# Layer 3: two row scans in one instruction, steps of 511 and half columns, decay in four fixed banks, another order of PE's pieces

## The chip, the cores and the metric

The kernel runs on one core of a Trainium2 chip, in float32 throughout. The metric is the device time of one launch in microseconds (us), the median of several runs. One further execution was recorded by the profiler; its page and its trace are what the profile lines below come from. Engines are named as the profile does: PE is TensorE's matmul and PEld its weight load, DVE is VectorE, ACT is ScalarE, POOL is GpSimd, SP is the engine that issues most DMAs.

## The reference

Four residual layers work on x of 2 x 192 x 96 x 96, each on a group-normalised x: a deformable convolution block, a Laplacian with a 1x1 convolution, a two-way WKV block, and a Mamba block. Only the last is touched by the change:

```
xz = x_flat @ W_in.T;  x_in, z_gate = split(xz)          # 192 -> 2 x 384 channels
x_conv = silu(causal depthwise conv of 4 taps(x_in) + conv_b)
dt, B_ssm, C_ssm = split(W_x x_conv, [12, 16, 16])
delta = softplus(W_dt dt + 2 b_dt);   A = -exp(A_log)    # A: 384 channels x 16 states
for t:  h = exp(delta_t A) * h + (delta_t x_conv_t) B_t ;  y_t = sum over the 16 states of h C_t
y = (y + D x_conv) * silu(z_gate);   x = x + W_out y
```

The loop over t has 9216 steps in each of two batches; h starts at zero in each batch.

## The kernel before

Layer 3 cuts each batch into 18 steps `s` of 512 columns (positions t), 36 in all. The 384 x 16 rows of h are worked in 12 groups `q` per step (counter `k` = 12 s + q), each of 4 x 128 rows: partition p holds a state and one of 8 channels, `r` = 0 to 3 picks a further channel. For one group:

- `load` (L2322): SP loads `bu`, 128 x (4 x 512), from the DRAM tile `ud` that holds delta * x_conv; each of its rows goes to 16 partitions. `times_b` (L2330, POOL) multiplies it by the rows `bs` of B.
- `steps_of` (L2339, PE): four matmuls of 32 x 512, one for each 32-row part of the array, spread delta over the states, each into a PSUM bank of the pool `da` of five. `decay` (L2353, ACT): exp of it, in place, with the scale `nA`.
- `scan` (L2363, DVE): four scans of 512 columns, h = da * h + bu, that start from a column of `state` (0 at a batch's start). `keep` (L2370, ACT) copies the last column to `state`.
- `times_c` (L2386, DVE) multiplies three of the rows by `cc`, the rows of C in PSUM; `times_c_aside` (L2397, POOL) multiplies the fourth. `sum_of` (L2410, PE) sums over the states into `acc`, two groups later; `skip` (L2404) adds D x_conv; `gate` (L2423, DVE) makes `y` at every fourth group.

What prepares a step are generators. `early` (two steps ahead): `xn` on ACT, 6 projections `w_in` of two matmuls each (L2231), evicted to `xi` or `zs`, 3 convolutions of four `taps` matmuls (L2251), evicted to `us`, then Silu of `zs` and `us`. `late` (one step ahead): `wx` (L2266) to `xd`, whose rows go through DRAM to `bs` and `cs`; 3 `wdt` matmuls (L2290), each evicted twice, to `du` and `dl`; then softplus: Exp and Identity on ACT, L2300 on DVE, Ln on ACT, L2303, L2305 and L2307 on POOL, and the store of `ud`. `output` (for the step before): load of `xr`, two times three `w_out` matmuls (L2435), each followed by an addition on DVE (L2443), and the store. All of these matmuls share one PSUM bank, `pe`; with `cc`, `acc` and the five `da` that is eight.

The order on PE, ACT, DVE and POOL is the order of the program (`manual_schedule`): nothing overtakes on an engine's queue. The loop over `k` draws the next part from a generator at given q: `AHEAD` ahead of the sums and scans, `BEHIND` after the scans and between `steps_of` and `decay` of the next group. ACT has to load a table of functions when it passes between Exp, Ln and Silu (a row of its own, 1.28 us). SP issues DMAs in its own order, each when its wait is over.

Of the kernel before, what the change touches and what calls it, by code (L numbers as in the profile page):

```python
# [9 lines left out]
ALU = mybir.AluOpType  # L10
# [53 lines left out]
class Net:  # L64
# [2021 lines left out]
    def layer3(self, x, out, stats):  # L2086
# [4 lines left out]
        T = 512  # L2091
        NC = HW // T
# [5 lines left out]
        with ExitStack() as ctx:  # L2098
# [81 lines left out]
            pa = ctx.enter_context(tc.tile_pool(name="l3a", bufs=5, space=PSUM))  # L2180
# [9 lines left out]
            tail = wp.tile([P, ND, 3], F32, name="tail")  # L2190
            ctx.enter_context(
# [9 lines left out]
            steps = [(b, c) for b in range(B) for c in range(NC)]  # L2201
            ns = len(steps)
            got = {}

            def bank():
                return ps.tile([P, T], F32, name="pe")

            def early(s):

                b, c = steps[s]  # L2210
                xt = sb.tile([CH, 2, T], F32, name="xt")
                nc.sync.dma_start(out=xt, in_=halves(x[b])[:, :, c * T : (c + 1) * T])
                xn = s1.tile([CH, 2, T], F32, name="xn")
# [5 lines left out]
                us = s3.tile([P, ND, T], F32, name="us")  # L2219
                zs = s3.tile([P, ND, T], F32, name="zs")  # L2220
                xi = s1.tile([P, ND, T + 3], F32, name="xi")
                got[s] = {"us": us, "zs": zs}
                if c == 0:
                    nc.gpsimd.memset(tail, 0.0)
                nc.scalar.copy(xi[:, :, 0:3], tail)
                yield

                def project(at):
                    pe = bank()
                    for k in range(2):  # L2230
                        nc.tensor.matmul(  # L2231
                            pe, w_in[:, k, at : at + P], xn[:, k], start=k == 0, stop=k == 1
                        )
                    return pe

                for d in range(ND):
                    pe = project(d * P)
                    yield
                    nc.scalar.copy(xi[:, d, 3:], pe)  # L2239
                    if d == ND - 1:  # L2240
                        nc.scalar.copy(tail, xi[:, :, T : T + 3])
                    yield
                for d in range(ND):
                    pe = project(DI + d * P)
                    yield
                    nc.scalar.copy(zs[:, d], pe)
                    yield
                for d in range(ND):
                    pe = bank()
# [371 lines left out]
```

## Time and profile before

| | |
|---|---|
| median of 3 runs | 10371.55 us (10369.88 to 10373.33) |
| the profiled execution | 10376.11 us, span 10373.9 us |
| busy in the span: PE, DVE, ACT, POOL | 88%, 80%, 58%, 67% |
| layer 3's preparation, first projection to first scan | 7063.7 to 7182.8 us |
| its loop, first scan to the last product `hc` | 7182.8 to 10358 us |
| its end, to the end of the span | 15.5 us |
| in 7182.4 to 10360: PE, DVE, ACT, POOL busy | 2985, 2925, 1902, 2815 of 3178 us |

A line of the page's groups gives the source line, the engine, the operation, output and inputs with their shapes, the count, then busy us, mean ns of one, and the idle time just before them with what ended most of it. An fp32 matmul is recorded as two passes. In the rows by stages, PEclk is the share of TensorE's full clock that was granted.

### The profile page before, as it was taken

To read this page: it belongs to the slowest core of one execution; us is meant where nothing else is said; L and a number is where in the kernel's file an instruction comes from. 1 tells how busy PE (TensorE), PEld (TensorE's weight loads), DVE (VectorE), ACT (ScalarE), POOL (GpSimd) and SP (SyncE) were. 2 spreads that over 40 slices of the span, in tenths; PEclk is the share of its full clock that TensorE was granted. 3 is DMA by queue.
4 is the path that set the end of the run, shared out by engine and by line. 5 is a ranking of instruction groups with operands and counts; after the bars stand their busy time and mean duration, and the time that the engine had idled before them with its cause. 6 is when DMAs were issued, how large, how long until landed. Compare 5 with 4: busy or idle time off the path is not lost.

```text
span 10373.9 us, 220102 instructions
## 1 busy us (share of the span) xinstructions
PE 9171.9 (88%) x87142; PEld 5308.5 (51%) x87142; DVE 8299.5 (80%) x8704; ACT 6000.9 (58%) x11216; POOL 6976.3 (67%) x5591
## 2 busy tenths in 40 slices
PE   4799999999889999999776677887999999999998
PEld 3588787778777888888622222222222222222222
DVE  5788878788677777777655789883999999999998
ACT  0366666666566777777500178663666666656664
POOL 1466766766566666666501268773888888898887
PEclk8899999999999999999888788886888888888887
DMA  8455555555434545555434344433777777777776
GB/s 149 93 138 135 139 137 135 137 133 139 111 96 130 137 135 139 137 137 138 113 122 132 128 146 152 128 110 93 171 170 169 175 172 171 174 171 172 171 169 147
DMA packets 695775, 1465.03 MB, mean 141 GB/s; under 512 B 250912, under 2 KB 400676, under 8 KB 638340
## 3 DMA queue, kind: packets, MB, share of 16 engines
q1 hardware_dynamic: 481900, 1264.08, 47.2%
q0 software_dynamic: 104000, 133.19, 5.4%
q10 hardware_dynamic: 108840, 53.57, 2.0%
q8 instruction: 697, 11.42, 0.5%
q14 instruction: 338, 2.77, 0.1%
HBM read 871.06 MB, written 381.46 MB: 121 GB/s over the span
## 4 chain that ended last, share of the span: by engine, by line
PE 26%; DVE 14%; ACT 6%; issue 3%; POOL 1%; DMA 0%; SPq 0%; DVEq 0%; ACTq 0%; POOLq 0%
DVE h L2363 6%; PE da L2339 5%; PE pe L2231 4%; ACT da L2353 3%; PE acc L2410 3%; PE pe L2251 3%; PE pe L1523 2%; DVE opq L1882 2%; PE pe L2266 2%; DVE hc L2386 1%; PE pe L1515 1%; PE v L1732 1%; PE acc L2404 1%; PE pm L1997 1%; ACT t L1858 1%
## 5 line engine op out<-in xcount | busy, mean ns | idle before, releaser
L581 DVE TENSOR_TENSOR sp<-h 128x2304 f32<-128x2304 f32 x790 | 2161.5, 2769 | 37.9 <-ACT h L560 37.9
L2363 DVE TENSOR_TENSOR_SCAN h<-da,state,bu 128x512 f32<-128x512 f32 x1632 | 1960.3, 1264 | 223.8 <-ACT da L2353 203.6
L2330 POOL TENSOR_TENSOR bu<-bu,bs 128x2048 f32<-128x2048 f32 x432 | 1954.1, 4523 | 16.7 <-DMA bu<-ud 16.3
L605 ACT COPY st<-pt 128x512 f32<-128x512 f32 (+1 forms) x2370 | 1213.7, 515 | 1093.9 <-PE pt L597 1020.6
L597 PE MATMUL pt<-ident,sp 128*128 128x128 f32 x14220 | 1675.3, 276 | 83.0 <-DVE sp L581 38.9
L603 DVE COPY st<-pt 128x512 f32<-128x512 f32 x1580 | 1064.1, 687 | 818.0 <-PE pt L597 804.9
L597 PEld LDWEIGHTS pt<-ident,sp 128*128 128x128 f32 x14220 | 1566.1, 142 | 165.2 <-issue 97.6
L551 POOL TENSOR_TENSOR h<-u,step 128x1152 f32<-128x1152 f32 (+1 forms) x474 | 1095.4, 2330 | 678.6 <-DVE u L524 480.9
L569 POOL DMA_DIRECT2D xw<-xp_d x2500 | 1390.1, 622 | 187.9 <-PE pt L648 83.7
L2353 ACT ACTIVATE da<-da,nA 128x512 f32<-128x512 f32 x1728 | 1044.8, 661 | 649.2 <-PE da L2339 647.5
L648 PE MATMUL pt<-st,xw 64*32 64x288 f32 (+1 forms) x30000 | 1095.7, 370 | 146.9 <-DVE st L603 65.8
L674 ACT COPY val<-pt 128x288 f32<-128x288 f32 (+1 forms) x3000 | 957.7, 404 | 288.4 <-PE pt L648 260.4
L776 PE MATMUL pf<-main,wd 126*64 126x128 f32 (+1 forms) x17064 | 990.1, 274 | 9.1 <-DMA far_m<-val 8.7
L776 PEld LDWEIGHTS pf<-main,wd 126*64 126x64 f32 x17064 | 917.6, 141 | 155.4 <-issue 149.2
L2339 PE MATMUL da<-dl,spread 32*128 32x512 f32 x3456 | 957.3, 696 | 15.4 <-DVE h L2363 7.2
L648 PEld LDWEIGHTS pt<-st,xw 64*32 64x32 f32 x30000 | 546.1, 106 | 561.9 <-ACT val L674 171.5
L2386 DVE TENSOR_TENSOR hc<-h,cc 128x1536 f32<-128x1536 f32 x432 | 748.1, 1732 | 0.0
L797 PE MATMUL pf<-more,wl 118*64 118x144 f32 (+5 forms) x11592 | 730.7, 276 | 2.9 <-DMA more<-far_l 2.3
L797 PEld LDWEIGHTS pf<-more,wl 118*64 118x64 f32 (+1 forms) x11592 | 663.0, 136 | 70.4 <-issue 64.3
L2231 PE MATMUL pe<-xn,sb_w_in 96*128 96x512 f32 x864 | 571.7, 796 | 123.5 <-ACT xi L2239 63.2
L2397 POOL TENSOR_TENSOR hp<-h,cs 128x512 f32<-128x512 f32 x432 | 550.8, 1275 | 144.7 <-PE da L2339 84.1
L2339 PEld LDWEIGHTS da<-dl,spread 32*128 32x128 f32 x3456 | 297.1, 195 | 646.9 <-DVE h L2363 410.8
(341 smaller groups left out, 13006.1 us busy)
## 6 DMA issues: line engine op xcount, KB each, us to landing
bu<-ud SPq DMA_DIRECT2D x432, 1024.0 KB
main<-val SPq DMA_DIRECT2D x2016, 91.1 KB
far_l<-val SPq DMA_DIRECT2D x288, 324.0 KB
xw<-xp_d POOLq DMA_DIRECT2D x2500, 26.0 KB
far_m<-val SPq DMA_DIRECT2D x288, 162.0 KB
xt<-x_d SPq DMA_DIRECT2D x108, 384.0 KB
half_d<-hv SPq DMA_DIRECT2D x54, 768.0 KB
hv<-half_d SPq DMA_DIRECT2D x54, 768.0 KB
```

The costliest lines, as they stand in the source:

```text
L551: nc.gpsimd.tensor_tensor(hs, u[:, :, 8 * KK * l : 8 * KK * l + n].unsqueeze(3).to_broadcast([P, 2, n, WS]), con["step"].unsqueeze(1).unsq ...
L569: nc.gpsimd.dma_start(out=xw[e * WN : (e + 1) * WN, i], in_=xp_d[y : y + WS, x : x + WS, e * CM // 2 : e * CM // 2 + XW],)
L581: nc.vector.tensor_tensor(sp.rearrange("p s (y x) -> p s y x", x=WS), hy.unsqueeze(3).to_broadcast([P, n, WS, WS]), hx.unsqueeze(2).to_bro ...
L597: nc.tensor.transpose(pt[:, q], sp[:, 2 * (q0 + q) : 2 * (q0 + q) + 2].rearrange("p e w -> p (e w)"), self.ident,)
L605: nc.scalar.copy(st[:, q0 : q0 + m], pt[:, :m])
L648: nc.tensor.matmul(to, xw[e * WN : (e + 1) * WN, win, g * CG : g * CG + 32], sts[pair][e * WN : (e + 1) * WN].rearrange("p s (r c) -> p s ...
L776: nc.tensor.matmul(place(cv, m, 2 - t // 3, 2 - t % 3, None, 0), con["wd"][:, cv, t, m * CO : (m + 1) * CO], blocks(took, 1, rows), start= ...
L797: nc.tensor.matmul(place(cv, m, 2 * cv if alone else 1 - cv, 2 - t, h, 1 - alone,), con["wl"][lanes, slot, t, m * CO : (m + 1) * CO], bloc ...
L2330: nc.gpsimd.tensor_tensor(bu, bu, got[s]["bs"].unsqueeze(1).to_broadcast([P, 4, T]), ALU.mult)
L2339: nc.tensor.matmul(das[r], spread[at, v].rearrange("p n e -> p (n e)"), got[s]["dl"][at, i], start=True, stop=True, tile_position=(32 * r, 0),
L2353: nc.scalar.activation(da, da, AF.Exp, scale=nA[:, 4 * q + r : 4 * q + r + 1])
L2363: nc.vector.tensor_tensor_scan(h[:, r], got[s]["da", q][r], bu[:, r], init, ALU.mult, ALU.add)
```

## The change

- Steps have 511 columns; 9216 = 17 x 511 + 529, and the 529 become steps of 265 and 264, the first two of batch 0 and the last two of batch 1. There are 38 steps and 456 groups.
- `bu` and `h` get a column in front of each row. `load` puts the DMA's data behind it and has ACT copy `state` (or zeros) into it. The decay tiles are two fixed PSUM tiles of two banks each, whose first columns are set to zero once. A scan over a pair of rows, 2 x 512 columns, thus starts each row anew from its carried state. In short steps each row is scanned by itself, with the column in front.
- `steps_of`, `decay` and `scan` work on a pair `j` of rows; the pair's two banks become free with its own scan.
- Two banks `pe` instead of one. The generators become single pieces with fixed places (q, j): the table `BETWEEN`. A piece is a matmul group and its eviction; it stands ahead of the pair's `steps_of`. `early` is split into `start` (q=1), the 12 pieces of `WHOLE` from (2, 1) to (8, 0), and `silus` (q=9); `late` into `rows`, `widths`, `powers` (q=2), `rest` and `logs` (q=3), `less`, `plus`, `inputs` (q=5, 6, 7); `output` into `old` (load of `xr`, q=8), the matmuls behind the pair's `steps_of` at q=9 and 10, and both additions at q=10. `inner` and `outer` are the projections to `xi` and `zs`, `conv` half a convolution (two taps).
- `hc` has two buffers instead of three, `y` two instead of one.

The diff, cut to its core:

```diff
-        T = 512
-        NC = HW // T
+        TM = 511
+        short = HW % TM + TM
+        whole = [TM] * (HW // TM - 1)
...
-            pa = ctx.enter_context(tc.tile_pool(name="l3a", bufs=5, space=PSUM))
+            pb = ctx.enter_context(tc.tile_pool(name="l3b", bufs=2, space=PSUM))
...
+            none = wp.tile([P, 4], F32, name="none")
+            nc.vector.memset(none, 0.0)
+            decays = [ps.tile([P, 2, 512], F32, name=f"da{j}") for j in range(2)]
+            for da in decays:
+                nc.vector.memset(da[:, :, :1], 0.0)
...
+            halved = [short - short // 2, short // 2]
+            steps = []
+            for b in range(B):
+                t0 = 0
+                for T in halved + whole if b == 0 else whole + halved:
+                    steps.append((b, t0, T))
+                    t0 += T
...
+            def bank(m=P, T=TM):
+                return pb.tile([P, 512], F32, name="pe")[:m, :T]
...
+            def conv(s, d, half):
+                T = steps[s][2]
+                if half == 0:
+                    got[s]["conv"] = bank(T=T)
+                pe = got[s]["conv"]
+                for j in (2 * half, 2 * half + 1):
+                    nc.tensor.matmul(
+                        pe, taps[:, d, j], got[s]["xi"][:, d, j : j + T], start=j == 0, stop=j == 3
+                    )
+                if half == 0:
+                    return None
+                return lambda: nc.scalar.activation(
+                    got[s]["us"][:, d], pe, AF.Identity, bias=cb[:, d : d + 1]
+                )
+
+            def silus(s):
+                for t in (got[s]["zs"], got[s]["us"]):
+                    nc.scalar.activation(t, t, AF.Silu)
...
             def load(k):
                 s, q, i, v = where(k)
-                t = sc.tile([P, 4, T], F32, name="bu")
+                T = steps[s][2]
+                t = sc.tile([P, 4, TM + 1], F32, name="bu")[:, :, : T + 1]
                 one = got[s]["ud"][i, v]
                 nc.sync.dma_start(
-                    out=t, in_=bass.AP(one.tensor, one.offset, [[0, NST], [4 * T, 8], [1, 4 * T]])
-                )
+                    out=t[:, :, 1:],
+                    in_=bass.AP(one.tensor, one.offset, [[0, NST], [4 * T, 8], [1, 4 * T]]),
+                )
+                nc.scalar.copy(t[:, :, 0], none if steps[s][1] == 0 else state[:, q])
                 got[s]["bu", q] = t
 
             def times_b(k):
                 s, q, _, _ = where(k)
-                bu = got[s]["bu", q]
+                bu = got[s]["bu", q][:, :, 1:]
                 nc.gpsimd.tensor_tensor(
-                    bu, bu, got[s]["bs"].unsqueeze(1).to_broadcast([P, 4, T]), ALU.mult
-                )
-
...
+            def steps_of(k, j):
                 s, q, i, v = where(k)
-                das = [pa.tile([P, T], F32, name="da") for _ in range(4)]
-                for r in range(4):
+                for r in (2 * j, 2 * j + 1):
                     at = slice(32 * r, 32 * r + 32)
                     nc.tensor.matmul(
-                        das[r],
+                        decays[j][:, r % 2, 1 : 1 + steps[s][2]],
                         spread[at, v].rearrange("p n e -> p (n e)"),
                         got[s]["dl"][at, i],
                         start=True,
                         stop=True,
                         tile_position=(32 * r, 0),
                     )
...
-            def scan(k):
+            def scan(k, j):
                 s, q, _, _ = where(k)
-                h = sb.tile([P, 4, T], F32, name="h")
-                bu = got[s]["bu", q]
-                for r in range(4):
-                    init = 0.0 if steps[s][1] == 0 else state[:, q, r : r + 1]
-                    nc.vector.tensor_tensor_scan(
-                        h[:, r], got[s]["da", q][r], bu[:, r], init, ALU.mult, ALU.add
-                    )
-                got[s]["h", q] = h
+                T = steps[s][2]
+                if j == 0:
+                    got[s]["h", q] = sb.tile([P, 4, TM + 1], F32, name="h")[:, :, : T + 1]
+                h, bu = got[s]["h", q], got[s]["bu", q]
+                if T == TM:
+                    two = slice(2 * j, 2 * j + 2)
+                    parts = [
+                        [t.rearrange("p r t -> p (r t)") for t in (h[:, two], decays[j], bu[:, two])]
+                    ]
+                else:
+                    parts = [
+                        (h[:, 2 * j + r], decays[j][:, r, : T + 1], bu[:, 2 * j + r]) for r in range(2)
+                    ]
+                for to, da, one in parts:
+                    nc.vector.tensor_tensor_scan(to, da, one, 0.0, ALU.mult, ALU.add)
...
-                hc = s3.tile([P, 3, T], F32, name="hc")
+                T = steps[s][2]
+                hc = sb.tile([P, 3, TM], F32, name="hc")[:, :, :T]
...
+            def old(s):
+                b, t0, T = steps[s]
+                xr = s1.tile([CH, 2, TM], F32, name="xr")[:, :, :T]
+                nc.sync.dma_start(out=xr, in_=halves(x[b])[:, :, t0 : t0 + T])
+                got[s]["xr"] = xr
...
+            WHOLE = [(outer, 0), (inner, 0), (inner, 1), (inner, 2), (outer, 1)]
+            WHOLE += [(conv, 0, 0), (conv, 0, 1), (outer, 2), (conv, 1, 0), (conv, 1, 1)]
+            WHOLE += [(conv, 2, 0), (conv, 2, 1)]
+            BETWEEN = {
+                (0, 1): (1, rows),
+                (1, 0): (1, widths, 0),
+                (1, 1): (1, widths, 1),
+                (2, 0): (1, widths, 2),
+            }
+            slots = [(2, 1), (3, 0), (3, 1), (4, 0), (4, 1), (5, 0), (5, 1)]
+            slots += [(6, 0), (6, 1), (7, 0), (7, 1), (8, 0)]
+            for slot, piece in zip(slots, WHOLE):
+                BETWEEN[slot] = (2, *piece)
...
+            def between(s, q, j):
+                if (q, j) not in BETWEEN:
+                    return None
+                ahead, make, *args = BETWEEN[q, j]
+                return make(s + ahead, *args) if s + ahead < ns else None
+
+            adds = []
             for k in range(nk):
                 s, q, _, _ = where(k)
-                if q == 0 and s + 1 < ns:
-                    running["late"] = late(s + 1)
-                if q == 2 and s:
-                    running["out"] = output(s - 1)
-                if q == 3 and s + 2 < ns:
-                    running["early"] = early(s + 2)
-                if q in AHEAD:
-                    go(AHEAD[q])
-                    go(AHEAD[q])
+                more = s + 1 < ns
+                if q == 1 and s + 2 < ns:
+                    start(s + 2)
                 if k >= 2:
                     sum_of(k - 2)
                 if q == 0 and s:
                     rows_c(s)
-                scan(k)
-                if q in (4, 5):
-                    go("out")
-                if k + 1 < nk:
-                    steps_of(k + 1)
-                if q in BEHIND:
-                    go(BEHIND[q])
-                if k + 1 < nk:
-                    decay(k + 1)
-                if q in BEHIND and BEHIND[q] != "out":
-                    go(BEHIND[q])
-                if q == 3:
-                    go("late")
-                    go("early")
+                for j in range(2):
+                    scan(k, j)
+                for j in range(2):
+                    now(between(s, q, j))
+                    if k + 1 < nk:
+                        steps_of(k + 1, j)
+                        decay(k + 1, j)
+                    if j == 1 and s and q in (9, 10):
+                        adds.append(output(s - 1, q - 9))
                 times_c(k)
                 if k >= 2 and (k - 2) % NV == NV - 1:
                     gate(k - 2)
-                if q in (4, 5, 6, 7):
-                    go("late")
-                if q == 11:
-                    go("early")
+                if q == 2 and more:
+                    powers(s + 1)
+                if q == 3 and more:
+                    rest(s + 1)
+                    logs(s + 1)
+                if q in (5, 6, 7) and more:
+                    (less, plus, inputs)[q - 5](s + 1)
+                if q == 8 and s:
+                    old(s - 1)
+                if q == 9 and s + 2 < ns:
+                    silus(s + 2)
+                if q == 10:
+                    for add in adds:
+                        add()
+                    adds = []
...
```

## The prediction

> **What bounds the kernel now.** I read the page's groups first, then the stages, then the DVE timeline of one step, then the waits. Only layer 3 changes; its loop runs from the first scan (7182.8 us) to the last products (10358 us), 36 steps of 88.2 us.
>
> The page's costliest groups, those of layer 3's loop (columns: count, busy us, mean ns, then idle before):
>
> ```profile
> L2363 DVE TENSOR_TENSOR_SCAN h<-da,state,bu 128x512 f32<-128x512 f32 x1632 | 1960.3, 1264 | 223.8 <-ACT da L2353 203.6
> L2330 POOL TENSOR_TENSOR bu<-bu,bs 128x2048 f32<-128x2048 f32 x432 | 1954.1, 4523 | 16.7 <-DMA bu<-ud 16.3
> L2353 ACT ACTIVATE da<-da,nA 128x512 f32<-128x512 f32 x1728 | 1044.8, 661 | 649.2 <-PE da L2339 647.5
> L2339 PE MATMUL da<-dl,spread 32*128 32x512 f32 x3456 | 957.3, 696 | 15.4 <-DVE h L2363 7.2
> L2397 POOL TENSOR_TENSOR hp<-h,cs 128x512 f32<-128x512 f32 x432 | 550.8, 1275 | 144.7 <-PE da L2339 84.1
> ```
>
> Four scans, one product on DVE, two products on GpSimd per group k; 12 k make a step. The loop as one stage (length; busy us of PE, PEld, DVE, ACT, POOL; granted clock; DMA share; GB/s):
>
> ```profile
> 7182.40:10360.00 3177.60, 2985.16 (x9660) 889.88 (x9660) 2925.23 (x2372) 1902.42 (x3157) 2815.24 (x967) 0.85 0.73 170
> ```
>
> DVE is busy 92%, GpSimd 89%, PE 94% with part of that waiting, DMA 73%. DVE holds the end, closely followed. One stretch of a step on DVE (start, length, idle before):
>
> ```profile
> 8014.05 4.80 DVE L2363 TENSOR_TENSOR_SCAN h<-da,state,bu 128x512 f32<-128x512 f32 x4
> 8018.77 0.66 DVE L2443 TENSOR_TENSOR xr<-pe,xr 96x512 f32<-96x512 f32 x1
> 8019.35 1.74 DVE L2386 TENSOR_TENSOR hc<-h,cc 128x1536 f32<-128x1536 f32 x1
> 8021.01 0.68 DVE L2423 TENSOR_TENSOR y<-acc,zs 128x512 f32<-128x512 f32 x1
> 8021.61 4.80 DVE L2363 TENSOR_TENSOR_SCAN h<-da,state,bu 128x512 f32<-128x512 f32 x4
> 8026.33 1.73 DVE L2386 TENSOR_TENSOR hc<-h,cc 128x1536 f32<-128x1536 f32 x1
> 8032.31 4.81 DVE L2363 TENSOR_TENSOR_SCAN h<-da,state,bu 128x512 f32<-128x512 f32 x4 [4.25 <-ACT da L2353]
> ```
>
> From start to start four scans take 4.72, `hc` 1.65, `xr` 0.58, `y` 0.60, `rest` 1.67. A step is 12 x 6.37 + 3 x 0.60 + 2 x 0.58 + 1.67 = 81.0 us of DVE work and about 7 us of holes; the 4.25 us is the largest. What made it is in the stages of 3.3 us before it (same columns):
>
> ```profile
> 8016.50:8019.80 3.30, 2.47 (x5) 0.84 (x6) 3.30 (x4) 3.27 (x6) 2.88 (x1) 0.89 0.36 88
> 8019.80:8023.10 3.30, 3.30 (x4) 0.92 (x4) 3.30 (x4) 0.84 (x2) 3.30 (x3) 0.50 0.92 231
> 8023.10:8026.40 3.30, 2.63 (x4) 1.17 (x4) 3.30 (x4) 0.68 (x2) 3.30 (x2) 0.50 0.80 211
> ```
>
> After `da` matmuls that trickled in one by one behind scans, the granted clock is 0.50; two projections of `early` (3.75 and 3.78 us instead of 1.98) run one after the other through the only `pe` bank, and `da` of the next group stands behind them in PE's queue.
>
> **Scan, part one of the sum.** 48 scans of 512 become 24 of 1024, with a constant start instead of `state`. The same scan with a constant start is in the trace: 1.198 us, against 1.264. DVE products of 512 and 1536 columns take 0.68 and 1.74, so 0.15 us of one is fixed; given that to the scan, 1.05 us for 512 columns is its stream. 1024 columns: 0.15 + 2.10 = 2.25 long, 2.17 from start to start (0.08 of each scan overlaps the next); upper end, no fixed part saved, 2.4; lower end 2.13. I take 2.20, between the worked value and two constant-start scans at 1.12. DVE per group 2 x 2.20 + 1.64 = 6.04; per step 12 x 6.04 + 4.6 = 77.1, 3.9 less than now.
>
> **GpSimd.** `times_b` and `times_c_aside` keep their size (511 for 512); they now start one column in, in rows of 511. The trace has such a product: layer 1's `pair`, 17 rows of 97 at offset 1, 1649 elements in 3145 ns, 1.91 ns each against 2.21 for `bu`. So nothing is added. From start to start 4.49 + 1.23 per group plus 3 x 3.39 (`less`, `plus`, `inputs`): 78.8 per step. GpSimd becomes the floor, above DVE's 77.1. It now loses about 7 us per step waiting for `ln` (7.16 idle at 8016.9); `logs` moves from q=4 to q=3, so `less` at q=5 finds it ready.
>
> **PE.** Four `da` (row tiles, 1.07 us on the chain of waits when all four banks are free) become two pairs, 1.0 each if a pair runs together (two passes of 0.43), 1.7 if not; I take 1.05, as four do run together. Start to start at full clock: 8 passes of `taps` 3.63, so 0.907 per matmul; sums 1.0. Per step 12 x (1.0 + 2.1) + 40 x 0.907 (12 projections, 12 `taps`, 3 each of `wx`, `wdt`, `skip`, 6 `w_out`, 1 `cc`) = 73.5. The 12 pieces now lie one per half group, q=2 to 8, over two banks. In q=3 to 7 PE needs 1.0 + 2.1 + 4 x 0.907 = 6.7 (7.6 with `skip` at q=6) against DVE's 6.04: by q=7 it is 3 us behind. A scan tolerates about 1.5 (a pair freed at 2.2, filled at 3.25, two exponentials 1.25, wanted at 6.04). Stall 1.5 us. GpSimd's three extra products end `hp` of q=6 at 27.0 us after scan q=4 began, where PE wants it at 25.7: 1.3, mostly the same time. Together 1.7. `hc` has two buffers instead of three, so the next `hc` also waits for these sums; it comes 2 us later than they do and pays nothing unless PE lags more.
>
> **ACT.** Ln with its two table loads (1.28 + 1.48 + 1.28) sits behind `rest` on DVE; counted from scan q=3 (`rest` done at 7.7) it ends at 10.5, then two small copies, an eviction of 0.58, the table back and two exponentials: 14.0 where scan q=5 wants 13.7. Stall 0.3. At q=1 `xn` (1.6) and two evictions of 1.38 precede exponentials: 0.5. The new column copy in `load` is a 0.19 us row (`state`), 12 per step, in ACT's 35 idle us; uncovered it would be 2.3. If it also waited for the load into its own tile it would still come after the landing.
>
> **The new wait.** `output` moves to q=9 and 10, behind `steps_of`; both `xr` additions stand on DVE in q=10 behind `hc`, ahead of the next scan. The second waits for three matmuls that start at 5.45 and end at 8.2, against 6.6 when DVE is there. 1.6 us per step; who waits is scan q=11 and with it everything.
>
> **Clock.** q=11 and the start of q=0 give PE 4 us of work in 8, the thin kind that preceded half clock above. If it falls there, `rows` takes 5.4 (5.35 at 8071.3) instead of 2.7 and the second scan of q=1 comes 4.4 late; if not, 0. I take 2.2. [...]
>
> A whole step: 77.1 + 1.7 + 0.3 + 0.5 + 1.6 + 2.2 = 83.4 us, between 81.2 and 85.6.
>
> **Loads.** `bu` was 128 packets of 8 KB, becomes 512 of 2044 B. Alone on the queue (7150 to 7165 us; packets, MB, share):
>
> ```profile
> q1 hardware_dynamic: 464, 3.41, 102.3%
> ```
>
> That is 227 GB/s, 4.62 us per load, 577 ns per 8 KB packet. The store of `ud` in 2 KB packets kept 200 GB/s: 154 ns each, so 512 take 4.9. Layer 0's packets of 1.8 KB on average took 107 ns: 3.4. DMA per step now 0.74 x 88.2 = 65, 9.8 of it other than `bu`; after 51 to 69 of 83. Hidden. SP's order moves too: the load of `xt` from q=3 to q=1, of `xr` from q=2 to q=8, the store from q=5 to q=10, at about 0.55 us of SP each and with the same bytes; `xt` stands behind one `bu` load and lands about 1.1 us into q=1, before ACT reaches `xn`. Nothing is charged; uncovered it would be 2 us. [...]
>
> **Short steps and ends.** Each batch gains a step: 265 and 264 instead of one, 38 in all. A short step on DVE: 48 x 0.62 (266 columns by the line above) + 12 x 0.88 + 2.6 = 43. Steps 0 and 1 must project whole steps meanwhile: 24 x 0.907 on top of 12 x 1.6 and some 8 smaller pieces, 50 of PE; I take 54 and 55. The last two: 45 and 44. Start: from 7063.7 to the first scan, 119 us, went `early`, `late`, `early` in series at half clock, each piece 3.78 + 0.67 through one bank. With 265 columns and two banks one `early` is 15 us (full clock) to 24 (half) instead of 45; between and behind them lie now 27 (Silu to Ln) and 6.6; halved, but for table loads of 1.28 each, 16 and 6. 7063.7 + 2 `early` + 22 gives a first scan at 7116 to 7134; I take 7125. The other way to it (three GpSimd products, store, load, `times_b`; 27 us now) stays shorter. The end (15.5 us after the last `hc`) has half the columns and two banks: 9.5.
>
> **Sum.** 7125 + 54 + 55 + 34 x 83.4 + 45 + 44 + 9.5 = 10168 us of span, against 10373.9. The profiled execution took 10376.1, 2.2 above its span; the median of the runs, 10371.6, lies 4.6 below it. 10168 + 2.2 - 4.6: 10165. A measurement of this kernel tells about 0.2%, 21 us, from no change.
>
> **Rivals.**
> - *GpSimd's floor is reached*: the stalls fall into each other, 79.3 per step. For it: GpSimd ran 67 us after 8016.9 with one hole of 0.24. Against: the q=10 wait is on DVE itself. 7332.5 + 34 x 79.3 - 2.4 = 10026. Chance 0.15.
> - *PE becomes the bound*: its clock stays at the present mean of 0.85; 73.5 / 0.85 = 86.5, with the q=10 wait growing, 87. 10288. For it: the thin stretch. Against: PE busy all through q=2 to 8, and the clock was 1.00 from 8030 to 8069. 0.15.
> - *The long scan saves nothing*: 2.40, 24 x 0.2 = 4.8 more; 88.2, 10329, still 0.4% faster through the short start. Against: the constant-start row. 0.05.
> - *Loads become the bound, slower than before*: place, the queue of `bu`; a step cannot be shorter than 12 loads + 9.8. The loop loses to before from 89.5 per step, which is 6.6 us per load, 44% over today's 4.62. At twice today's it is 121 per step, 11430. For it: four times the packets, none aligned, all reading the same rows. Against: 2 KB rows above. 0.10 slower.
> - The forecast, 0.55.
>
> The range, 10030 to 10320, leaves out the loads, the scan without saving and the lowest few hundredths of the first rival. Faster by over 0.2%: 0.85; within, where the last two rivals meet: 0.04; slower: 0.11.
>
> **What would show it.** Scan groups of 128x1024 near 2.25 us, 816 of them, with 192 short ones; DVE in a whole step busy about 77 of 83; the idle before scans mostly from ACT `da` at q=7, 8, 1; `xr` waiting for PE `pe` about 1.6 per step; GpSimd's wait for `ln` gone; the first scan near 7125; `bu` loads under 5.5 us each. Wrong if a load exceeds 6.6, if scans read over 2.35, if `bu` products read over 4.6, or if the clock's mean in the loop is under 0.85.

## The result: 5.8% slower, and the profile after

The changed kernel takes 10965.3 us (median of 4 runs, 10958.8 to 10969.6) against 10370.7 us (4 runs, 10356.7 to 10373.3): a ratio of 1.0576, 95% interval 1.0557 to 1.0594. The forecast was 10165, its range ended at 10320. The profiled execution took 10963.65 us, its span is 10961.8.

The same groups of layer 3's loop on the page of the changed kernel (columns as before; "+2 forms" are the short steps):

```profile
L2413 DVE TENSOR_TENSOR_SCAN h<-da,bu 128x1024 f32<-128x1024 f32 (+2 forms) x1008 | 1967.0, 1978 | 704.2 <-ACT da L2393 689.6
L2372 POOL TENSOR_TENSOR bu<-bu,bs 128x2044 f32<-128x2044 f32 (+2 forms) x456 | 1959.8, 4298 | 175.3 <-DMA bu<-ud 121.8
L2393 ACT ACTIVATE da<-da,nA 128x511 f32<-128x511 f32 (+2 forms) x1824 | 1159.4, 639 | 1059.6 <-PE da L2380 764.6
L2380 PE MATMUL da<-dl,spread 32*128 32x511 f32 (+2 forms) x3648 | 1269.3, 777 | 269.7 <-DVE h L2413 264.2
```

The two longest groups did not get dearer: the products of `bu` are as long as predicted (4.51 us for a whole step's), and all scans together take 1967 us instead of 2070 (the 1960.3 of the row shown before and 109.5 for the 96 that start from zero). PE's `da` matmuls did, from 957.3 to 1269.3 us, and the exponentials from 1044.8 to 1159.4. What grew is the idle time ahead of the scans, from 223.8 to 704.2 us, nearly all of it spent on the exponentials, which themselves wait 764.6 us for PE's `da`. So the scans now wait in a ring: a scan frees a pair of banks, PE fills it, ACT takes the exponential, the next scan waits; PE, with the pieces that stand ahead of each pair, is its slowest part. The 31 whole steps in the middle (from one `rest` to another) show how PE does it, as one stage of the kernel before and then of the changed one (length; busy us of PE, PEld, DVE, ACT, POOL; granted clock; DMA share; GB/s):

```profile
7391.90:10137.13 2745.23, 2589.63 (x8434) 777.42 (x8433) 2524.49 (x2048) 1668.55 (x2760) 2444.50 (x838) 0.86 0.74 171
```

```profile
7397.04:10688.24 3291.20, 3052.28 (x8452) 839.76 (x8452) 2586.23 (x1304) 1776.54 (x3134) 2443.94 (x839) 0.76 0.62 143
```

A step went from 88.56 to 106.17 us. DVE is busy 83.4 us of it (81.4 before), GpSimd 78.8 as before, PE 98.5 (83.5 before), and the granted clock fell from 0.86 to 0.76. The prediction's 73.5 us of PE work at full clock, divided by 0.76, is 96.7: PE is the busiest engine, with the work foreseen and a clock that was not. Whether it is also the bound is for the experiments.

One stretch of a step on DVE, on GpSimd and on PE (start, length, then idle before):

```profile
8551.48 2.29 DVE L2413 TENSOR_TENSOR_SCAN h<-da,bu 128x1024 f32<-128x1024 f32 x1 [0.52 <-ACT da L2393]
8553.87 1.75 DVE L2434 TENSOR_TENSOR hc<-h,cc 128x1533 f32<-128x1533 f32 x1
8555.54 5.73 DVE L2330 SCALAR_TENSOR_TENSOR du<-ln,du 128x1533 f32<-128x1533 f32 x1
8561.19 4.46 DVE L2413 TENSOR_TENSOR_SCAN h<-da,bu 128x1024 f32<-128x1024 f32 x2
...
8567.42 2.28 DVE L2413 TENSOR_TENSOR_SCAN h<-da,bu 128x1024 f32<-128x1024 f32 x1
8572.74 2.29 DVE L2413 TENSOR_TENSOR_SCAN h<-da,bu 128x1024 f32<-128x1024 f32 x1 [3.04 <-ACT da L2393]
```

```profile
8555.15 4.50 POOL L2372 TENSOR_TENSOR bu<-bu,bs 128x2044 f32<-128x2044 f32 x1
8562.86 3.42 POOL L2336 TENSOR_TENSOR ln<-ln,du 128x1533 f32<-128x1533 f32 x1 [3.21 <-ACT bu L2366]
```

```profile
8557.90 1.98 PE L2242 MATMUL pe<-xn,sb_w_in 96*128 96x511 f32 x4
8563.52 2.08 PE L2380 MATMUL da<-dl,spread 32*128 32x511 f32 x4 [3.64 <-DVE h L2413]
8565.53 3.78 PE L2242 MATMUL pe<-xn,sb_w_in 96*128 96x511 f32 x4
8569.23 2.07 PE L2380 MATMUL da<-dl,spread 32*128 32x511 f32 x4
```

`rest` takes 5.73 us instead of the 1.75 it took before. GpSimd's product began 0.39 us ahead of it, ends at 8559.65, and `rest` ends 1.6 us later, about its own length, as if it had stood still while the product ran. Behind it the scans come late, PE waits 3.64 us for a free pair, and then, at a granted clock of 0.50 (from 8561.50 to 8575.16 us), everything on PE takes twice as long: a pair 2.08 instead of 1.06, a projection 3.78 instead of 1.98. With the clock at half, two pairs, two pieces and the sums (2 x 2.0 + 2 x 3.7 + 1.9) are 13.3 us per group, twice what DVE needs, and the next scan waits 3.04. Where the clock is full (1.00 from 8575.16 to 8602.46 us), PE goes round in 6.93 us (the `w_in` of 8582.09 to the `taps` of 8589.02), 0.2 above the forecast.

### The profile page after: what moved, and what is told of

Read it like the earlier page. It is cut to its first block, busy times and chain, and to the rows that moved or that the text cites. A ratio compares the mean times of both kernels' runs of the same rounds, so it can differ in the third digit from the quotient of the medians.

```text
span 10961.8 us, 222839 instructions
## 1 busy us (share of the span) xinstructions
PE 9686.0 (88%) x87686; PEld 5429.5 (50%) x87686; DVE 8374.3 (76%) x8023; ACT 6171.4 (56%) x11850; POOL 6989.9 (64%) x5645
## 4 chain that ended last, share of the span: by engine, by line
PE 32%; DVE 12%; ACT 3%; issue 2%; POOL 2%; DMA 1%; SPq 0%; DVEq 0%; ACTq 0%; POOLq 0%
PE da L2380 7%; DVE h L2413 5%; PE pe L2242 5%; PE acc L2458 3%; PE pe L2269 3%; PE pe L2486 2%; PE pe L1523 2%; PE pe L2288 2%; DVE opq L1882 2%; PE acc L2452 1%; ACT da L2393 1%; PE pe L1515 1%; DVE hc L2434 1%; PE v L1732 1%; PE pm L1997 1%
## 5 line engine op out<-in xcount | busy, mean ns | idle before, releaser
L2413 DVE TENSOR_TENSOR_SCAN h<-da,bu 128x1024 f32<-128x1024 f32 (+2 forms) x1008 | 1967.0, 1978 | 704.2 <-ACT da L2393 689.6
L2372 POOL TENSOR_TENSOR bu<-bu,bs 128x2044 f32<-128x2044 f32 (+2 forms) x456 | 1959.8, 4298 | 175.3 <-DMA bu<-ud 121.8
L2393 ACT ACTIVATE da<-da,nA 128x511 f32<-128x511 f32 (+2 forms) x1824 | 1159.4, 639 | 1059.6 <-PE da L2380 764.6
L2380 PE MATMUL da<-dl,spread 32*128 32x511 f32 (+2 forms) x3648 | 1269.3, 777 | 269.7 <-DVE h L2413 264.2
L2445 POOL TENSOR_TENSOR hp<-h,cs 128x511 f32<-128x511 f32 (+2 forms) x456 | 553.4, 1214 | 621.0 <-DVE h L2413 611.4
L2380 PEld LDWEIGHTS da<-dl,spread 32*128 32x128 f32 x3648 | 348.6, 225 | 1066.4 <-DVE h L2413 514.2
L2434 DVE TENSOR_TENSOR hc<-h,cc 128x1533 f32<-128x1533 f32 (+2 forms) x456 | 761.4, 1670 | 97.9 <-PE acc L2458 58.7
L2242 PE MATMUL pe<-xn,sb_w_in 96*128 96x511 f32 (+2 forms) x912 | 632.2, 834 | 12.3 <-ACT xn L2228 6.7
```

The lines of the kernel that those rows point to most:

```text
L2242: nc.tensor.matmul(pe, w_in[:, k, at : at + P], got[s]["xn"][:, k], start=k == 0, stop=k == 1)
L2372: nc.gpsimd.tensor_tensor(bu, bu, got[s]["bs"].unsqueeze(1).to_broadcast([P, 4, steps[s][2]]), ALU.mult)
L2380: nc.tensor.matmul(decays[j][:, r % 2, 1 : 1 + steps[s][2]], spread[at, v].rearrange("p n e -> p (n e)"), got[s]["dl"][at, i], start=True, ...
L2393: nc.scalar.activation(da, da, AF.Exp, scale=nA[:, 4 * q + r : 4 * q + r + 1])
L2413: nc.vector.tensor_tensor_scan(to, da, one, 0.0, ALU.mult, ALU.add)
```

## The experiments

The table has every run: median and ratio to the kernel before, and from the profile of each, over those whole steps in the middle, the step, PE's busy time in it and the mean granted clock. The profile is of one execution, which can lie tens of us from the median (in e_light 100 us above it).

| run | us | ratio (95%) | step | PE busy | clock |
|---|---|---|---|---|---|
| before | 10371 to 10379 | 1 | 88.6 | 83.5 | 0.86 |
| after | 10965 | 1.0557-1.0594 | 106.2 | 98.5 | 0.76 |
| e_rest4 | 11177 | 1.0742-1.0781 | 112.6 | 104.1 | 0.74 |
| e_rest_one | 10885 | 1.0475-1.0511 | 103.6 | 96.0 | 0.78 |
| e_rest_scan | 10898 | 1.0478-1.0513 | 104.2 | 96.9 | 0.77 |
| e_fill | 10722 | 1.0308-1.0347 | 98.6 | 95.0 | 0.89 |
| e_fill_thin | 11215 | 1.0781-1.0817 | 113.5 | 110.6 | 0.72 |
| e_light | 10890 | 1.0451-1.0504 | 106.8 | 98.1 | 0.70 |
| e_pad | 11658 | 1.1212-1.1249 | 126.9 | 124.0 | 0.78 |
| e_pad32 | 11072 | 1.0647-1.0685 | 109.2 | 99.8 | 0.77 |
| e_four_scans | 10961 | 1.0543-1.0578 | 105.8 | 97.5 | 0.77 |
| e_together | 10963 | 1.0547-1.0582 | 105.5 | 79.4 | 0.79 |
| e_before_pairs | 10620 | 1.0217-1.0254 | 95.9 | 90.4 | 0.84 |
| e_before_banks | 10419 | 1.0029-1.0065 | 90.8 | 89.5 | 0.87 |
| e_lump | 10808 | 1.0371-1.0445 | 101.1 | 88.4 | 0.79 |
| e_rest_one_fill | 10695 | 1.0287-1.0340 | 96.3 | 92.0 | 0.92 |
| e_v1 | 10690 | 1.0263-1.0306 | 97.8 | 94.7 | 0.88 |
| e_v2 | 11289 | 1.0848-1.0913 | 115.7 | 114.7 | 0.84 |
| e_lump_rest | 10494 | 1.0097-1.0138 | 92.1 | 82.5 | 0.87 |
| e_all | 10565 | 1.0166-1.0200 | 94.3 | 86.8 | 0.88 |

The expectations weigh three theories. Theory 1: `rest` stands still beside GpSimd's product, and PE starves behind it. Theory 2: PE's pieces and its two pairs per group set the pace by the work that they are. Theory 3: the granted clock does.

### What `rest` costs

e_rest4 moves it (and Ln) to the group where it stood before:

```
-                if q == 3 and more:
+                if q == 4 and more:
                     rest(s + 1)
                     logs(s + 1)
```

> Whole steps take 105.4 us in the changed kernel, and rest in q=3 takes 5.7 instead of 1.75. Theory 1 (rest stands still while GpSimd's product of q=3 runs, and PE starves behind it): one group later GpSimd waits for ln, as it did before the change; rest falls to about 1.75 and a step by 4 to 8 us: 10690 to 10830. Theory 2 (PE's pieces and two da pairs per group set the pace, rest lies in their shadow): rest gets short, but a step falls by 1 us at most: 10930 to 10965. Theory 3 (the clock alone): a stretch at half clock behind rest goes with it, about 2 us per step: 10890.

```profile
L2330 DVE SCALAR_TENSOR_TENSOR du<-ln,du 128x1533 f32<-128x1533 f32 x29 | 50.8, 1750 | 0.0
```

```profile
POOL ln L2336 <- ACT bu L2366: 584.1, 31, 21.2
```

`rest` is short again, as its line in the groups by form between 7300 and 10500 us shows, and yet the kernel is 212 us slower than the changed one, which no theory expected. The waits (total, times, longest) tell why: GpSimd now stands 19 us in each step before `less`, which needs Ln (the wait is put down to a copy on ACT that stands near it), and behind `less` stand the `hp` and `bu` products. The price of waiting moved from DVE to GpSimd's queue. The run shows that the block depends on when `rest` runs, not that undoing it in this way pays. Two other edits keep Ln where it is:

```
e_rest_one:   nc.vector.scalar_tensor_tensor(du, du, 0.0, cc, ALU.mult, ALU.mult)
e_rest_scan:  rest(s + 1) at q == 3 behind the two scans, ahead of times_c
```

> In its old place in q=3, rest becomes du = (du x 0) x cc with cc in PSUM: same size and engine, one SBUF input instead of two; it leaves out the rounding term of the logarithm. Theory 1 (rest stands still because it reads two SBUF tiles while GpSimd's product reads SBUF): it takes 1.75 everywhere instead of 5.72 and a step loses 4 to 7 us: 10720 to 10830. If it stands still for another reason it still reads 5.7 and the time is 10965. If it gets short but lies in the shadow of PE's ring (theory 2): 10930 to 10965.

> rest of q=3 stands right behind the second scan and ahead of hc, at the moment where GpSimd begins to wait for that scan, instead of behind hc; it is the same instruction with two SBUF inputs. Theory 1 (it stands still only while GpSimd's product runs): it takes 1.75 to 3.0 instead of 5.72, and the time falls as with one SBUF input (10885): 10860 to 10910. If place does not matter: 5.7 and 10965.

```profile
L2334 DVE SCALAR_TENSOR_TENSOR du<-du,cc 128x1533 f32<-128x1533 f32 x30 | 52.4, 1746 | 0.0
```

With one input in SBUF and the other in PSUM it takes 1.746 us in the same place, where with both in SBUF it took 5.72: in these runs the second SBUF input is what blocks. Behind the scans it takes 2.40 on average with both inputs. The two runs save 80 and 67 us, 2.6 and 2.0 us per step, where 4.0 and 3.3 went out of `rest` itself; the remainder came back as other holes. Theory 1 holds for the block, and it explains about an eighth of the loss; the 10720 to 10830 us that were expected of it with one input were not reached.

### What the clock costs

e_fill puts matmuls of no use into the half groups of q=0 and 8 to 11 without a piece; e_fill_thin the same ones on 32 rows:

```
+  nc.tensor.matmul(bank(), taps[:, 0, 0], got[s]["us"][:, 0], start=True, stop=True)
e_fill_thin:  taps[:32, 0, 0], got[s]["us"][:32, 0], tile_position=(0, 0)
```

> One matmul of taps on us (128 rows, 511 columns, 0.91 us at full clock) into an unused pe bank in each of the half groups of q=0 and q=8 to 11 that have no piece, in steps 2 to 35: about 8 a step, 7 us of PE work added, the result of no use. Theory 2 with PE's work as such the bound: +7 us per step, 11200. Theory 3 (thin stretches of 32-row matmuls drop the clock to 0.50): the clock's mean over the loop rises from 0.75 to over 0.82 and a step gets 3 to 8 us shorter, 10690 to 10860, with more work. Theory 1: the clock behind rest is not touched by this, at most 4 us per step, 10830.

> The extra matmuls of the run with more work (10722), in the same slots, with the same columns and time of PE, but on 32 rows of the array instead of 128. If the clock goes by how long PE is busy, the same 10720. If it goes by how much of the array works (theory 3 in its strict form), the clock stays near 0.75 and the 7 us of work cost time: 10965 to 11300.

e_fill, its 2800 us in the loop, and e_fill_thin in the same stretch:

```profile
7400.00:10200.00 2800.00, 2697.14 (x8165) 751.05 (x8163) 2313.44 (x1190) 1625.04 (x2862) 2258.66 (x768) 0.89 0.70 153
```

```profile
7400.00:10200.00 2800.00, 2730.63 (x7104) 770.96 (x7102) 2059.50 (x1034) 1421.47 (x2493) 1948.74 (x669) 0.72 0.59 133
```

More work, 244 us less time, clock 0.89. The same time of PE on a quarter of the rows: 250 us more, clock 0.72. So the clock is a cause here and not only a sign, and in these two runs it didn't go by how long PE was busy. e_light takes 128-row work away, and e_pad and e_pad32 add work on other rows behind each pair:

```
e_light:  for j in (2, 3) if half == 0 else ():      # two of four taps
e_pad32:  at = slice(64 - 64 * j, 96 - 64 * j)       # e_pad: 64 rows
+         nc.tensor.matmul(spare[0][:, :TM], taps[at, 0, 0], got[s]["us"][at, 0], ..., tile_position=(at.start, 0))
```

> Two of the four taps of each conv are left out (the second half of conv is empty, so its output is wrong): six 128-row matmuls, 5.4 us of PE at full clock, less per step, all else the same. Theory 2 (PE's work as such is the bound): 5 to 8 us per step less, 10700 to 10800. Theory 3 (128-row work is what holds the clock up): the clock's mean falls below 0.76 and eats the saving: 10900 to 11100.

> Behind each pair of da matmuls (rows 0 to 63 or 64 to 127) stands one more matmul of taps on us on the other 64 rows, into the pe bank that the next piece overwrites; its result is of no use. It needs no data and can run beside the pair, so all 128 rows work in the 1.06 us that two tiles took. Theory 3 (the clock goes by how many rows work): the clock's mean over the loop over 0.88, a step of 90 to 97 us, 10430 to 10680. If only longer work of PE holds the clock: nothing, 10950 to 11000. If the third matmul does not run beside the pair: 24 x 0.5 us more and the 64 rows too few: 11100 or more.

> As the run with a third matmul behind each pair (11658, where it took 1.05 us of its own), but on 32 of the other rows, the size of the pair's own tiles, so that it can run beside them: three of four row tiles work. Theory 3 (working rows hold the clock): clock over 0.80 in the loop, 10500 to 10850, with no time of PE added. If the clock does not go by that: 10950 to 11000. If it does not run beside the pair either: 11500 to 11700.

e_light: 5.4 us less work per step at full clock, and in the profiled execution the clock is down to 0.70, PE is busy for the same 98 us and the time (10990) is no shorter than the changed kernel's. The median saves 76 us. Over the whole span each of its four executions has a lower clock (0.849 to 0.863) than those of the changed kernel (0.867 to 0.869). That speaks for the 128-row work as what held the clock in the changed kernel. The 64-row matmul of e_pad did not run beside the pair; it took 1.05 us of its own, and the run says nothing on rows. The 32-row one did, on PE's timeline:

```profile
8502.24 0.70 PE L2397 MATMUL da<-dl,spread 32*128 32x511 f32 x2
8502.25 0.69 PE L2229 MATMUL pe<-us,taps 32*128 32x511 f32 x1
8502.77 0.59 PE L2397 MATMUL da<-dl,spread 32*128 32x511 f32 x2
8502.79 0.59 PE L2229 MATMUL pe<-us,taps 32*128 32x511 f32 x1
```

Three row tiles at work, and the clock at 0.77: no better, and 106 us slower; between 8500 and 9500 us the exponentials wait 183 us for the extra matmul. So a third tile beside the pairs did not raise the clock by itself. The run does not refute that the clock goes by rows either, since the waits put new holes into PE's work.

The traces of the kernel before and of the changed one show what went with the clock. In both, between 7400 and 9990 us, it is 1.0 or 0.5, and every stretch at one of the two lasts a whole number of 3.413 us (in the changed kernel the half clock from 8561.50 to 8575.16 us four of them, the full clock behind it, to 8602.46 us, eight). Call such a length a window, and *row use* the share of the array's 128 rows on which passes run, as a mean over a window (an estimate from the records: a pass counts as its record less 0.135 us, and 32-row tiles that run together add up). While they run, a pair of `da` uses 0.5 of the rows, all four 1.0, a projection of 96 rows 0.75, `taps` 1.0. The two traces have 922 windows at full clock: all 168 with a row use of 0.42 or less are followed by half clock, and 1 of the other 754. They have 594 at half clock: all 165 with a row use over 0.825 are followed by full clock, and 6 of the other 429. The two limits are fitted to such windows. PE's busy share, with the best limit for it, is wrong after 111 of the 922; after the 594 no limit of it does better than to say that the clock stays at half, which is wrong 171 times. The mean row use is 0.72 in the kernel before and 0.68 in the changed one; 16% and 21% of their windows at full clock have 0.42 or less. In the stretch shown above, PE's hole of 3.64 us begins in a window of 0.37 (from 8558.09 us), and the next is at half clock; behind one of 0.98 with the `taps` (from 8571.74 us) the clock is full again. This is read from two traces; of the experiments, e_fill against e_fill_thin is the one that varies the rows and little else.

### Which part of the change does it

e_four_scans undoes the long scan alone, e_together issues the four `da` in one pass:

```
e_four_scans:  -  if T == TM:        +  if False:
e_together:    four_of(k + 1)   # rows 2, 3, 0, 1 behind both pieces, then both decay
```

> Every group scans four times 512 columns instead of twice 1024, all else as in the changed kernel. If DVE sets the pace (theory 1 away from its wait): four scans at 1.20 are 4.80 against 4.57, 0.23 x 12 = 2.8 us per step more, 11060. If the ring through PE sets it (theory 2): nothing, within 20 us of 10965, and the 0.23 comes out of the holes. If the long scan itself is the harm (its drain in front of hc): 1 to 2 us per step less, 10900 to 10930.

> The four da matmuls of a group are issued together, after both scans of the group before: 1.07 us of PE per group instead of 2.12, but the first scan of the next group then waits for 1.07 + 1.32 us (matmuls, two exponentials) less hc's 1.75: a hole of about 0.7 on DVE in each group. Theory 2 (PE's time for pairs is what is lost): 12.6 us less PE work per step against 8 us of holes that the step already has for other reasons: 92 to 98 us per step, 10510 to 10720. If PE does not set the pace (theories 1 and 3): 5 to 8 us per step more, 11130 to 11240.

The long scan gives nothing here: the time is the same to 4 us, and what the four scans take longer comes out of holes. e_together takes 19 us of PE's busy time out of a step and the step stays, which neither theory expected: it waits for the second scan instead, and PE, idle more often, keeps a clock of 0.79. So PE's time for pairs isn't the loss by itself; with both pairs behind the second scan the ring is as slow.

Two runs put one part each into the kernel before, a third takes the spread of the pieces back:

```
e_before_pairs:  scan(k); steps_of(k + 1, (0, 1)); sum_of(k - 2); steps_of(k + 1, (2, 3))
e_before_banks:  pa bufs=5 -> 4; pe from a pool of 2
e_lump:          now(between(s, q, 0)); now(between(s, q, 1)); then both steps_of, decay
```

> The kernel before, with one part of the change on PE alone: the four da matmuls of a group no longer stand together but two by two, with the sums of the group before last (1.0 us, all columns) between the pairs. Scans, banks, pieces and steps stay as before. If the pairs are what costs (da takes PE two passes of 1.06 instead of one of 1.07, half the row tiles at a time): the clock's mean falls from 0.85 to 0.80 or less and a step grows by 5 to 14 us: 10560 to 10860. If the pairs are harmless and the new order of the pieces or the four banks did it: within 40 us of 10376.

> The kernel before, with another part alone: two pe banks, and four da banks instead of five. If the shared pe bank was what PE waited for (0.7 to 1.07 us between two projections, at half clock in q=5 and 6): 1 to 3 us per step less and some 16 us off the start: 10250 to 10340. If the fifth da bank carried the scans: 0.3 to 1 us per group more, 10500 to 10800.

> The changed kernel with the two pieces of a group together ahead of both pairs, instead of one ahead of each. If the even spread of pieces is what thins PE's work: clock over 0.80, 10700 to 10900. If the ring sets the pace (a pair waits behind a piece): the first pair comes up to 1.8 us later in q=0 to 8, 9 to 16 us per step more, 11270 to 11500.

The pairs, with the sums between them, make the kernel before 2.35% slower, 245 us, with scans, banks, steps and `rest` as they were: PE is busy 6.9 us longer in a step that is 7.3 longer. The time is what was expected if the pairs cost; the mean clock, 0.84, did not fall to the 0.80 that was to go with it. (The sums moved too; pairs without them between were not tried.) Its steps now differ among themselves. Five of six in a row (columns as in the stages above):

```profile
7805.44:7893.85 88.41, 82.59 (x274) 23.28 (x273) 81.47 (x67) 54.11 (x90) 78.90 (x27) 0.92 0.74 172
7893.85:7989.81 95.96, 90.43 (x274) 24.98 (x273) 81.98 (x67) 54.20 (x90) 78.97 (x27) 0.84 0.69 158
8078.22:8178.18 99.96, 94.59 (x268) 25.54 (x268) 82.25 (x67) 53.06 (x87) 78.98 (x27) 0.78 0.69 154
8178.18:8269.60 91.42, 86.73 (x280) 24.67 (x277) 81.72 (x68) 55.66 (x93) 78.83 (x27) 0.91 0.70 162
8269.60:8381.90 112.30, 105.93 (x273) 28.60 (x272) 82.16 (x67) 54.18 (x90) 79.00 (x27) 0.71 0.58 136
```

(Between the second and the third one more step of 88.41 is left out.) The instructions are the same, and DVE, ACT and GpSimd are busy for nearly the same time; 88.4 us at a clock of 0.92, 112.3 at 0.71. The two banks (and with them the four for `da`) cost 44 us: neither the gain nor the loss of over 120 us that was expected. Two pieces together instead of one ahead of each pair save 157 us in the changed kernel, at a clock of 0.79.

### Do the causes add up

e_rest_one_fill joins the one-input `rest` and the extra matmuls; e_v1 a `rest` between the scans of q=4, `less` to `inputs` one group later, fewer extra matmuls, and the `xr` additions at q=10 and 11; e_v2 e_pad, e_rest_scan and those additions. e_lump_rest joins e_lump, e_rest_scan and the additions, with no work added; e_all adds the 128-row matmuls.

> The same together with the extra matmuls on us in the half groups without a piece (10722 alone). rest reads 4.2 us on average there, so if the two causes add up, 2.4 to 4 us per step come off: 10585 to 10640, at a clock of 0.90 or more over the loop. If rest's delay only made the clock fall (one cause in two clothes): 10680 to 10722.

> Everything that the runs so far blame, undone on top of the changed kernel: rest between the two scans of q=4, where GpSimd is about to wait; less, plus, inputs one group later, so that GpSimd does not wait for Ln; 128-row extra matmuls in q=8, 9, 11 and 0 only; the two xr additions in q=10 and 11. If the three causes are all there is: clock over 0.92, rest under 3, a step of 84 to 88 us, 10230 to 10370. If PE's pairs alone hold the step (theory 2), 92 or more: over 10500.

> Both of these together, and the two xr additions in q=10 and 11: the changed kernel with its full work and no extra time on PE. If clock and rest are the two causes and both are undone, a step at full clock and with rest at 1.75 (89 us where that came by chance in earlier runs, 2 of them xr's wait): 87 to 89 us, 10290 to 10420. If the clock still falls in every second step: 95 us, 10600.

> Three edits on the changed kernel, none of which adds work: both pieces of a group together (alone 10808), rest ahead of hc (alone 10898), the xr additions in q=10 and 11 (1.5 us a step by the profile). If the terms add: 10965 - 157 - 67 - 50 = 10690. If they are one cause (the clock) seen thrice: 10780 to 10810.

> The same with 128-row extra matmuls (one or two of 0.91 us) in q=8, 9, 11 and 0 of steps 2 to 35. If the clock is what is left: over 0.90 in the loop, steps near 90 us, 10400 to 10520. If the extra work only fills: 10690 or more. A step under 88 us, and so a kernel faster than the one before, would need both da pairs in one pass, and is not expected.

e_v1 and e_v2 missed by 320 and 870 us; e_v2 because its extra matmuls turned out to cost PE time. `rest` and the clock overlap: on top of the extra matmuls the one-input `rest` gives 27 us where alone it gave 80. But the three edits of e_lump_rest gave 471 us where 274 was the sum, the 50 for the additions being an estimate: the scans wait less for the exponentials, and the clock stays at 0.87. Why the terms add up to more than their sum was not taken apart.

```profile
L2413 DVE TENSOR_TENSOR_SCAN h<-da,bu 128x1024 f32<-128x1024 f32 x758 | 1692.4, 2274 | 349.0 <-ACT da L2393 265.7 <-POOL hp L2445 65.5 <-POOL bu L2372 17.8
L2330 DVE SCALAR_TENSOR_TENSOR du<-ln,du 128x1533 f32<-128x1533 f32 x31 | 73.7, 2379 | 0.0
```

(Groups by form between 7300 and 10200; the scans wait 349.0 us there, 265.7 of it for the exponentials.) There extra matmuls only cost time (e_all). No version beat the kernel before. The nearest, e_lump_rest, is 1.2% behind it and still has the pairs; that the pairs are those 1.2% is likely from e_before_pairs and was not tried.

## Why the prediction was wrong

Its sum against the profile: first scan 7114.8 (forecast 7125), step 0 79.1 (54), step 1 66.8 (55), 34 whole steps 105.4 on average (83.4), the last two 57.1 and 50.8 (45, 44), end 8.8 (9.5). The whole steps are 750 of the 794 us missed, the short ones 55, the start won 10.

- **The step that failed is the price of PE: the clock, and with it PE's stalls.** The clock was charged as one possible event of 4.4 us per step, weighted by half, and PE's stalls at full clock as 1.7. Holes were to be 6.3 us per step (83.4 less 77.1); they are 22.7 (106.17 less 83.43). The rival "PE becomes the bound" had the right mechanism and formula, 73.5 divided by the clock. It took the clock of before, 0.85, as given, though with the change it fell (0.86 to 0.76 over the whole steps): a pair of `da` uses half of the rows where four used all (mean row use 0.68 instead of 0.72), and PE waits for each pair. The forecast's own condition, a clock mean under 0.85, came true at 0.75 over the loop. The clock isn't all of it. e_lump_rest has 0.87 and a `rest` of 2.4 us and still takes 92.1 us a step, 8.7 over the forecast; e_rest_one_fill has 0.92 and takes 96.3, about 7 of it the added matmuls. So the 1.7 us for PE's stalls was too small at a clock like the one of before, too.
- **`rest` was costed at 1.67 by its row before** and moved one group. There it meets GpSimd's product: 5.72, the largest part of DVE's 6.3 us above the forecast. With one SBUF input it took 1.746 in the same place (e_rest_one). In the kernel before, `rest` didn't show it, because GpSimd was idle, waiting for `ln`, when it ran (in one step `rest` takes 1.75 us from 8012.38 us, and GpSimd is idle for 7.16 us up to 8016.92).
- **The scan was mis-sized a little.** 2.28 us each instead of 2.25, and 4.57 from the first scan to `hc` instead of 4.40, since `hc` starts 0.1 us after the last scan and not inside it: 2 us per step. That is half of the 3.9 us which the long scan was to bring; e_four_scans shows that the remainder was worth nothing in this ring.
- **`hc` with two buffers** was to pay nothing unless PE lags more. PE does, and `hc` now waits 58.7 us in all for the sums, where it waited for nothing before (first the kernel before, then the changed one):

```profile
L2386 DVE TENSOR_TENSOR hc<-h,cc 128x1536 f32<-128x1536 f32 x432 | 748.1, 1732 | 0.0
L2434 DVE TENSOR_TENSOR hc<-h,cc 128x1533 f32<-128x1533 f32 (+2 forms) x456 | 761.4, 1670 | 97.9 <-PE acc L2458 58.7
```

- **GpSimd's wait for `ln`** was to go. It is 205.9 us in 37 waits: Ln on ACT waits for `rest`, and `rest` is late.
- **What held:** the wait of `xr` at q=10 (1.46 against 1.6), the size of the hole around `rows` at half clock (3.3 to 4.0 us ahead of the second scan of q=1 in 31 of the 34 whole steps, 4.4 forecast, of which the sum took half as a chance), `bu` products (4.51), the shorter start and end, and the loads. Of them:

```profile
q1 hardware_dynamic: 144451, 281.84, 61.8%
```

That is the load queue between 8000 and 10000 us: 0.618 x 2000 x 16 / 144451 is 137 ns per packet of 1.95 KB, 4.4 us for the 512 of a load (an estimate), where 577 ns for 8 KB gave 4.62. (The forecast's 154 ns for a packet of 2 KB doesn't fit the 200 GB/s beside it, which makes 164; nothing hangs on it.) The rival of the loads falls.

## What to carry to other kernels

Matmuls on a pair of row tiles cost PE as much time here as on four (1.06 us against 1.07): splitting them to free banks earlier doubles the passes, and in a ring of engines that share banks the doubled passes are paid at whatever clock the new pattern is granted. Treat the clock as an outcome of the change (here 0.76 instead of 0.86): look for stretches in which few rows of the array work, and price PE at both 1.0 and 0.5, the two shares in these traces, before believing any slack. When an instruction with two SBUF inputs is moved, look up what GpSimd does at the new place (`rest` took 5.72 us beside its product, 1.75 where it was idle), and when its consumer is moved along, who stands behind that.

## What the runs showed of the hardware

The granted clock stayed at half although PE worked: in e_before_pairs, 45.5 us at 0.50 with PE busy 43.5 us of them and no hole on PE over 0.7 us:

```profile
8276.60:8322.10 45.50, 43.47 (x79) 11.33 (x75) 24.23 (x20) 11.48 (x23) 35.09 (x12) 0.50 0.55 127
```

PE ran 32-row `da`, sums, `skip` and 96-row projections in turn there. The row use of the 14 windows from 8273.3 to 8321.1 us was 0.57 to 0.83 (the estimate from above). The stage from 8322.10 to 8325.60 us had a clock of 0.66, the next one 1.00. In the traces of the kernel before and of the changed one, half clock followed all 168 windows at full clock with a row use of 0.42 or less, and full clock all 165 at half clock with one over 0.825; 1 of 754 and 6 of 429 of the others changed too. 128-row matmuls in the thin stretches went with a mean clock of 0.89 instead of 0.76 (e_fill), 32-row ones with 0.72 (e_fill_thin), a third tile beside each pair with 0.77 (e_pad32).

A 64-row matmul did not overlap with 32-row ones on other rows (e_pad: 1.05 us each on its own, PE busy 124.0 us a step instead of 98.5), a 32-row one did (e_pad32: it starts 0.01 us behind the pair's first pass).
